# Four copies of x into the output spread over the first units, the last behind a column gather, and the third tile's gather ahead of spreading the weights

## The chip, the core and the metric

The kernel runs on one core of a Trainium2 chip. Times are device microseconds of that core for one whole execution. Engines are TensorE (PE, its weight loads PEld), VectorE (DVE), ScalarE (ACT), GpSimd (POOL) and SyncE (SP). SP, ACT and POOL issue DMA transfers; indirect ones (gathers, and adds into rows of the output) come from POOL.

## The reference

4,096 tokens of 256 numbers go through a mixture of experts with a residual. Eight experts, each a three-layer network (256 to 512 to 512 to 256), two of them per token by a gate; cut to what matters:

```python
xn = rms_w * (x * rsqrt(mean(x * x) + EPS))
gate = xn @ wg_W + wg_b + (genre_embed @ gg_W + gg_b)
topk_w, topk_i = top_k(softmax(gate), 2)
cw = sum(one_hot(topk_i, E) * topk_w[..., None], axis=-2)      # a weight per token and expert
h1 = relu(einsum('bsh,ehm->bsem', x, W1) + b1)
h2 = relu(einsum('bsem,emn->bsen', h1, W2) + b2)
out_e = einsum('bsen,enh->bseh', h2, W3) + b3
return x + einsum('bseh,bse->bsh', out_e, cw)
```

## The kernel before, in words

Only the chosen pairs of token and expert are computed. Tokens lie as 128 partitions with 32 columns; the first 8 columns are part A, the other 24 part B. The gate of part A is computed first, and from it eight tiles of 128 tokens, one for each expert: **units 0 to 7** (E is 8). While these run, VectorE works out the gate of part B, sorts the remaining pairs into tiles by expert, and makes up units of four, two or one tiles, **unit 8 (E) and following**. How many units of which size there are is chosen at run time among prepared programs; the first ones have four tiles.

Each tile needs its rows of x (an indirect gather by token number into `xg`, `xgE` or a part of `big`), the gate weights of its tokens (a gather of 8 numbers per token into `cg`, from the table `cwdA` or `cwdR` that the kernel has written to DRAM: the *column gather*, `gather_cw`), and the expert's weights. After layer 3, `give` multiplies by the token's weight, adds the bias times that weight (`bc`, made by `scaled` from `b3_sb` and `cg`), and an indirect DMA adds the rows into the output (L1328). The output must hold x before: one copy for part A's rows of x (`our[:, 0:NA]`, 1,024 KB, in step 0) and four of 768 KB for part B (`fill`, L1425). Units 0 to 7 add into rows of part A alone and are independent of the four; the first add of unit 8 waits for all of them.

Order is written out by hand (`manual_schedule`): each engine runs its instructions in the order of the program text, and waits on semaphores. `head_step(u)` runs units 0 to 6: layer 1, the transposes of the next tile (L931), a piece of the sorting, layer 3 of the unit before, layer 2. `step(7)` and then `step_fast(u)` run the rest. In those, layers 1 and 2 of a unit with two tiles or more, and layer 3 of four, are computed by a recursion with seven block products instead of eight (classes `Fast` and `Wide`: `p` are matmuls, L1156 and L1246; `c11`, `c12`, `c22` at L1168, L1171, L1174 join products on VectorE; `mix` and `fold` make the sums of blocks; `r1`, `r21`, `r22` are the activations, L1177; copies out of PSUM are L1165 and L1255). `step_fast(u)` overlaps the end of unit u - 1 with the beginning of u. Its first act on VectorE is `scales(u - 1)`, which copies the unit's own columns out of `cg` (L1006); then comes `c22` of layer 2 of unit u - 1.

Queues around the change: SP issues the weights of units 0 to 7 in order (L461), three units ahead, then weights of unit 8 and later whose expert is read from memory (`stream_1`, `stream_3`), the bias rows `b3_sb`, the copies, and for each unit from 9 on the store and reload that reorder its rows (`stow`, L903, and `shuffle`, L910). POOL issues the gathers, the writing of the weight tables (`spread`, L441 to L444) and the output adds. The x gathers of the first three tiles come before step 0; those of tiles 0 and 1 before the table `cwdA` is written, that of tile 2 after it.

Of the kernel before, what the change touches and what calls it, by code (L numbers as in the profile page):

```python
# [52 lines left out]
def kernel(  # L53
# [17 lines left out]
    nc = tc.nc  # L71
    V = nc.vector
    P = 128
    B, S, H = x.shape
# [44 lines left out]
    def buf(pool, shape, name, dt=F32):  # L119
        return pool.tile(shape, dt, tag=name, name=name)  # L120
# [764 lines left out]
            fetches.append(fetch(xgR[u % 2][:, k], xrows, b))  # L885

    NCG = 16
    cgR = buf(run, [P, NCG, E], "cg")

    def gather_cw(u):  # L890
        for k, b in enumerate(tiles(u)):
            cg = cgs[b] = cgR[:, turn_of(u, k) % NCG]
            fetch(cg, (cwdA if b < E else cwdR)[:, :], b)

    xT = buf(run, [P, HC, SLOTS, BT], "xT")
    shs = gTf.rearrange("p (s k f) -> p s k f", s=SLOTS, k=P // SQ)
# [81 lines left out]
    def stream_3(u, engine=mybir.EngineType.Activation):  # L978
        e = expert(u, engine)
        QUEUES[engine].dma_start(w3r[u % RING], W3[e].rearrange("e (c p) h -> p (e c) h", p=P))  # L980
# [385 lines left out]
    def head_step(u, more):  # L1366

        if u + 3 < E:
            gather(u + 3)
        for k in range(3 * u, min(3 * u + 3, E)):  # L1370
            gather_cw(k)
        table(GC * (NCH - 1) * (u == E - 2))
        layer1(u)
        if u == 0:
            load_weights(u + RING, (0,))
            fills.append(nc.sync.dma_start(our[:, 0:NA, :], xr[:, 0:NA, :]))
            load_weights(u + RING - 1, (2,))
            load_weights(u + RING, (1,))
            nc.sync.dma_start(b3_sb[:, 2:4], b3[2:4].unsqueeze(0).to_broadcast([P, 2, H]))
            third_part()  # L1380
        elif u + RING < E:
            load_weights(u + RING, (0,))
        if u == 0:
            pass
        else:
            transpose_x(u + 1)
            stage_1(u + 1)
            if u == E - 2:
                while not fetched:
                    more(1000000)  # L1390
            elif u != 2:
                more(3200)
            if u > 1:
                scaled(u - 1, "A")
            layer3(u - 1)
            if u - 1 + RING < E:
                load_weights(u - 1 + RING, (2,))
            if u + RING < E:
                load_weights(u + RING, (1,))
            if u == 1:  # L1400
                nc.sync.dma_start(b3_sb[:, 4:E], b3[4:E].unsqueeze(0).to_broadcast([P, E - 4, H]))
        table(GC * (u == E - 3))
        if u == 0:
            layer2(u, {1: last_upright, 2: lambda: transpose_x(1)})
            stage_1(1)
            more(3200)
        else:
            more(3200)
            layer2(u)
        if u == 1:  # L1410
            scaled(0, "A")
        if u == E - 2:
            stream_3(E, mybir.EngineType.SP)
            stream_1(E + 1, mybir.EngineType.SP)
            stow(E + 1)
            shuffle(E + 1)
            give(u - 2)
        if u >= 1 and u != E - 3:
            give(u - 1)
        if u == E - 3:  # L1420
            stream_1(E, mybir.EngineType.SP)

    def fill(k):
        i = NA + k * (NB // NF)
        f = nc.sync.dma_start(our[:, i : i + NB // NF, :], xr[:, i : i + NB // NF, :])  # L1425
        for a in sum(adds, []):
            tc.declare_no_dep(f.ins, a.ins, reason="the first E tiles hold tokens of the first part alone")
        fills.append(f)

    def fetches_of(u, last):  # L1430
# [6 lines left out]
    def step(u, last):  # L1437
# [38 lines left out]
        if u == E - 1:  # L1476
            stream_1(E + 2, mybir.EngineType.SP)
            stream_3(E + 1, mybir.EngineType.SP)
            for k in range(NF):
                fill(k)  # L1480
        give(u - 1)
        for _ in folds:
            pass
# [1 line left out]
    def step_fast(u, last):  # L1485

        if u == E:
            transpose_x(u)
        far = fetches_of(u, last)
        follows = u + 1 < last  # L1490
        if follows:
# [189 lines left out]
    with tc.manual_schedule():  # L1681
        first_part()
        gather(0)
        other_loads()
        gather(1)
        second_part()
        pA.spread(cwdA, pA.cw8, 0)
        gather(2)
        other = rest()

        def routing(ns):
            while ns > 0:
                c = next(other, None)
                if c is None:
                    break
                ns -= c

        stage_1(0)
        for u in range(E - 1):
            head_step(u, routing)  # L1700
        for _ in other:
            pass
        for u in range(E - 1, CUT):
            if u == CUT - 2:
                _, (arm,) = nc.values_load_multi_w_load_instructions(
                    nex[0:1, 0:1],
                    min_val=0,
                    max_val=len(ARMS) - 1,
                    skip_runtime_bounds_check_because="the number of a shape of the tail",
                )  # L1710
            elif u == CUT - 1:
                tc.switch_hint({e: arm for e in ENGS}, len(ARMS), "tail")
            steps(u, u + 1, E + NQT + 1)
# [43 lines left out]
```

## Time and profile before

| | before |
|---|---|
| time, median of 3 runs | 452.51 us (452.5 to 453.68) |
| time of the profiled execution | 452.19 us |
| its span, first to last instruction | 450.5 us |
| TensorE busy | 440.3 us (98%) |
| VectorE, ScalarE, GpSimd busy | 368.3, 240.4, 279.8 us |
| moved by DMA | 78.89 MB, 175 GB/s in the mean |
| granted TensorE clock | 0.997 |

Times in the profile are us from the first instruction. A line of the timeline gives start, duration, engine, line of the program, what is written and read, how many instructions, and in brackets how long the engine was idle before and who ended that. A line of a stretch gives its bounds and length, then busy time and count of TensorE, its weight loads, VectorE, ScalarE and GpSimd, the granted clock, the busy share of the DMA engines and GB/s. A line of the DMA list gives what is written and read, the queue, the count, the size and the median us from issue to landing.

### The profile page before, as it was taken

The numbers are of one execution on the slowest core, as the hardware profiler recorded it, in microseconds if no ns is written. First come the engines' busy times: TensorE is split into PE (matmuls) and PEld (weight loads), VectorE is DVE, ScalarE is ACT, GpSimd is POOL, SyncE is SP. The second block draws the span as 40 slices with busy tenths as digits, with TensorE's granted clock in tenths as the row PEclk, the third lists the DMA queues.
The fourth block names the chain that finished last, engine by engine and source line by source line (L and its number), as shares of the span: only waits on it lengthen the run. The fifth ranks groups of instructions, "written<-read, shape, count | busy, mean of one in ns | idle before, by whom it ended". The sixth has DMA issues, their size and how long they took to land. (4 is left out here: it accounts for less than half of the span.)

```text
span 450.5 us, 9264 instructions
## 1 busy us (share of the span) xinstructions
PE 440.3 (98%) x2967; PEld 409.6 (91%) x2967; DVE 368.3 (82%) x964; ACT 240.4 (53%) x569; POOL 279.8 (62%) x234
## 2 busy tenths in 40 slices
PE   8999999999899999999999999999999999999995
PEld 7699999987889898989999999999999889999994
DVE  6897996586897979798988988887977878889962
ACT  5745544345556464728365555563454465655561
POOL 6855436756778878577675647588547456664223
PEclk9999999999999999999999999999999999999998
DMA  8799999495766758374655555567756645766312
GB/s 309 279 350 390 368 368 336 127 316 184 184 173 144 165 110 206 68 171 107 134 125 122 122 120 122 120 152 157 149 136 141 151 133 115 179 172 166 71 18 46
DMA packets 75871, 78.89 MB, mean 175 GB/s; under 512 B 34975, under 2 KB 64002, under 8 KB 75684
## 3 DMA queue, kind: packets, MB, share of 16 engines
q1 hardware_dynamic: 49264, 43.29, 30.3%
q0 software_dynamic: 14912, 17.60, 22.4%
q10 hardware_dynamic: 11636, 17.32, 12.2%
q8 instruction: 25, 0.41, 0.4%
q14 instruction: 34, 0.28, 0.2%
HBM read 62.73 MB, written 20.12 MB: 184 GB/s over the span
## 5 line engine op out<-in xcount | busy, mean ns | idle before, releaser
L1328 POOL DMA_INDIRECT out_dram<-ys,idxR x59 | 95.7, 1622 | 87.2 <-DVE ys L1327 41.7
L1177 ACT ACTIVATE hid<-hid,bb 128x256 f32<-128x256 f32 (+12 forms) x152 | 72.7, 528 | 21.7 <-DVE hid L1174 10.7
L1156 PE MATMUL pb<-hid,big 128*128 128x256 f32 (+7 forms) x456 | 83.3, 326 | 0.0
L864 POOL DMA_INDIRECT cg<-cwdR,idxR x59 | 66.5, 1126 | 18.0 <-issue 17.4
L1156 PEld LDWEIGHTS pb<-hid,big 128*128 128x128 f32 x456 | 71.4, 191 | 4.7 <-issue 0.8
L1278 PE MATMUL pb<-w3r,hid 128*128 128x256 f32 (+1 forms) x256 | 60.7, 381 | 0.0
L1165 ACT COPY q1s<-pb 128x512 f32<-128x512 f32 (+7 forms) x57 | 27.2, 477 | 60.9 <-PE pb L1156 60.3
L1156 PE MATMUL pb<-mixB,big 128*128 128x256 f32 (+7 forms) x304 | 55.5, 326 | 1.1 <-DVE hid L1174 1.1
L1165 ACT COPY big<-pb 128x512 f32<-128x512 f32 (+7 forms) x57 | 27.2, 477 | 51.9 <-PE pb L1156 51.9
L1156 PE MATMUL pb<-hotA,big 128*128 128x256 f32 (+7 forms) x304 | 52.3, 325 | 0.0
L1278 PEld LDWEIGHTS pb<-w3r,hid 128*128 128x128 f32 (+1 forms) x256 | 46.2, 189 | 6.1 <-issue 0.8
L1156 PEld LDWEIGHTS pb<-mixB,big 128*128 128x128 f32 x304 | 47.8, 191 | 4.0 <-DVE hid L1174 1.5
L1156 PEld LDWEIGHTS pb<-hotA,big 128*128 128x128 f32 x304 | 47.2, 191 | 2.7
L1156 PE MATMUL pb<-mixX,iotx 128*128 128x256 f32 (+7 forms) x228 | 46.3, 326 | 0.0
L864 POOL DMA_INDIRECT xgE<-in_x_dram,idxR x31 | 35.2, 1135 | 12.2 <-issue 8.2
L1156 PEld LDWEIGHTS pb<-mixX,iotx 128*128 128x128 f32 x228 | 37.1, 191 | 2.5 <-ACT q1s L1165 0.2
L864 POOL DMA_INDIRECT big<-in_x_dram,idxR x28 | 32.4, 1157 | 8.5 <-issue 7.3
L1177 ACT ACTIVATE hid<-pb,bb 128x256 f32<-128x256 f32 (+7 forms) x76 | 27.6, 414 | 14.7 <-PE pb L1156 11.7
L1156 PE MATMUL pb<-xT,w1r 128*128 128x256 f32 (+7 forms) x152 | 30.8, 325 | 0.0
L1057 PE MATMUL pb<-hid,w2a 128*128 128x128 f32 x256 | 30.4, 276 | 0.0
L1057 PEld LDWEIGHTS pb<-hid,w2a 128*128 128x128 f32 x256 | 29.9, 192 | 0.3
L919 DVE STREAM_TRANSPOSE xT<-gTs 128x256 f32<-128x256 f32 x55 | 29.0, 629 | 0.0
(341 smaller groups left out, 822.6 us busy)
## 6 DMA issues: line engine op xcount, KB each, us to landing
w3r<-in_L_cond_W_dram ACTq DMA_DIRECT2D x17, 512.0 KB, 5.6
w2a<-in_L_cond_W_dram SPq DMA_DIRECT2D x8, 1024.0 KB, 14.3
w1r<-in_L_cond_W_dram ACTq DMA_DIRECT2D x16, 512.0 KB, 3.8
w1r<-in_L_cond_W_dram SPq DMA_DIRECT2D x11, 512.0 KB, 10.0
w3r<-in_L_cond_W_dram SPq DMA_DIRECT2D x10, 512.0 KB, 11.2
big<-in_x_dram SPq DMA_DIRECT2D x8, 512.0 KB, 6.2
gTs<-scr SPq DMA_DIRECT2D x7, 512.0 KB, 4.6
out_dram<-in_x_dram SPq DMA_DIRECT2D x4, 768.0 KB, 9.4
```

Of the source, the lines that this page charges most:

```text
L864: return nc.gpsimd.indirect_dma_start(out=dst, out_offset=None, in_=src, in_offset=bass.IndirectOffsetOnAxis(ap=index(b), axis=0), bounds_ ...
L919: V.transpose(xT[:, :, s0 + k, :].rearrange("p c (b k) -> p k c b", b=SQ), shs[:, s0 + k].rearrange("p k (a c) -> p k c a", a=SQ),)
L1057: nc.tensor.matmul(ph, lhsT=w2[:, m, ts(n, P)], rhs=hid[0][:, m, 0:BT], start=(m == 0), stop=(m == MC - 1))
L1156: nc.tensor.matmul(bank[:, ts(n, self.w)], lhsT=w[:, c, ts(n, P)], rhs=x[:, c], start=new and n == 0 and c == 0, stop=n == HB - 1 and c == ...
L1165: nc.scalar.copy(self.q[(1, 6, 5).index(k)], self.tall(self.X if k == 5 else self.U))
L1177: nc.scalar.activation(out, src, AF.Relu, bias=ww[self.u][1][:, self.l, n : n + 1])
L1278: nc.tensor.matmul(sums(u, k)[0 : cols.stop - cols.start], lhsT=hid[1][:, n, cols], rhs=w3[:, n, :], start=(i == 0), stop=(i == MC - 1))
L1328: add = nc.gpsimd.indirect_dma_start(out=orows, out_offset=bass.IndirectOffsetOnAxis(ap=index(b)[0:n], axis=0), in_=y[0:n], in_offset=None ...
```

## The change

Four edits, all of order. The four copies `fill(0)` to `fill(3)`, before issued one behind the other at the end of `step(7)`, go to the end of `head_step(5)`, into `head_step(6)`, to the old place in `step(7)`, and to the head of `step_fast(8)`; the last waits until the last of unit 8's four column gathers has landed. The bias rows of experts 4 to 7, one load in step 1, become two loads, in steps 2 and 4. The x gather of the third tile goes ahead of writing `cwdA`. The amount of data and the computation are the same.

```diff
     def gather_cw(u):
         for k, b in enumerate(tiles(u)):
             cg = cgs[b] = cgR[:, turn_of(u, k) % NCG]
-            fetch(cg, (cwdA if b < E else cwdR)[:, :], b)
+            columns[u] = fetch(cg, (cwdA if b < E else cwdR)[:, :], b)
...
-            if u == 1:
-                nc.sync.dma_start(b3_sb[:, 4:E], b3[4:E].unsqueeze(0).to_broadcast([P, E - 4, H]))
+            if u in (2, 4):
+                nc.sync.dma_start(b3_sb[:, u + 2 : u + 4], b3[u + 2 : u + 4].unsqueeze(0).to_broadcast([P, 2, H]))
...
         if u == E - 2:
             stream_3(E, mybir.EngineType.SP)
+            fill(1)
             stream_1(E + 1, mybir.EngineType.SP)
...
         if u == E - 3:
             stream_1(E, mybir.EngineType.SP)
+            fill(0)

     def fill(k):
...
+        if k == NF - 1:
+            tc.add_manual_dep(
+                f.ins,
+                columns[E].ins.name,
+                mybir.DependencyInfo(mybir.DependencyClass.Sync, mybir.DependencyReason.DATA),
+                reason="the weight columns of the first unit go first",
+            )
         fills.append(f)
...
             stream_3(E + 1, mybir.EngineType.SP)
-            for k in range(NF):
-                fill(k)
+            fill(2)
         give(u - 1)
...
         if u == E:
             transpose_x(u)
+            fill(3)
         far = fetches_of(u, last)
...
         second_part()
+        gather(2)
         pA.spread(cwdA, pA.cw8, 0)
-        gather(2)
         other = rest()
```

How the rows move. First SP, from unit 8's third weights on (`w3r_88`; `ebt` is the number of the expert, `scr` the scratch of store and reload, `w1r_82`, `w1r_83` and `w3r_86` weights of units 9 and 10). Before:

```order
L980 DMA w3r_88<-in_L_cond_W_dram 128x4x256
L963 TENSOR_LOAD ebt
L976 ISA
L976 DMA w1r_82<-in_L_cond_W_dram 128x1024
L903 DMA scr_186<-big 128x16x64
L910 DMA gTs<-scr_186 128x4x256
```

and further down

```order
L976 DMA w1r_83<-in_L_cond_W_dram 128x1024
L963 TENSOR_LOAD ebt
L980 ISA
L980 DMA w3r_86<-in_L_cond_W_dram 128x4x256
L1425 DMA out_dram<-in_x_dram 128x1536 x4
L903 DMA scr_187<-xgE 128x16x64
L910 DMA gTs<-scr_187 128x4x256
```

In the change, from unit 8's first weights (`w1r_84`) on:

```order
L977 DMA w1r_84<-in_L_cond_W_dram 128x1024
L1428 DMA out_dram<-in_x_dram 128x1536
L964 TENSOR_LOAD ebt
L981 ISA
L981 DMA w3r_88<-in_L_cond_W_dram 128x4x256
L1428 DMA out_dram<-in_x_dram 128x1536
L964 TENSOR_LOAD ebt
L977 ISA
L977 DMA w1r_82<-in_L_cond_W_dram 128x1024
L904 DMA scr_186<-big 128x16x64
```

and where all four stood (with what each row waits for: `DMAHW` is a landing of SP's or ACT's transfers, `DMASW` one of POOL's):

```order
L964 TENSOR_LOAD ebt
L981 ISA
L981 DMA w3r_86<-in_L_cond_W_dram 128x4x256 [waits DMAHW2_49,PE_49]
L1428 DMA out_dram<-in_x_dram 128x1536 [waits DMAHW3_49]
L1428 DMA out_dram<-in_x_dram 128x1536 [waits DMAHW4_49,DMASW0_49]
L904 DMA scr_187<-xgE 128x16x64 [waits DMASW4_49,DMASW5_49,DMASW3_49,DMAHW5_49,DMASW2_49,Pool_49]
```

Two of the copies went up between the weights of units 8 and 9. Two still stand together; the second has a wait for a landing of POOL's, the column gather, and unit 10's store and reload stand behind it.

On POOL, the start of the gathers (`xg_209` to `xg_211` are the rows of tiles 0 to 2, then of 3 to 5). Before:

```order
L864 DMA xg_209<-in_x_dram,idxA 128x256
L864 DMA xg_210<-in_x_dram,idxA 128x256
L441 TENSOR_TENSOR cw8A<-ohA,denA 128x64
L442 TENSOR_TENSOR wA<-ohA,d2A 128x64
L443 TENSOR_TENSOR cw8A<-cw8A,wA 128x64
L444 DMA cwdA<-cw8A 128x64
L864 DMA xg_211<-in_x_dram,idxA 128x256
```

In the change:

```order
L864 DMA xg_209<-in_x_dram,idxA 128x256
L864 DMA xg_210<-in_x_dram,idxA 128x256
L864 DMA xg_211<-in_x_dram,idxA 128x256
L441 TENSOR_TENSOR cw8A<-ohA,denA 128x64
L442 TENSOR_TENSOR wA<-ohA,d2A 128x64
L443 TENSOR_TENSOR cw8A<-cw8A,wA 128x64
L444 DMA cwdA<-cw8A 128x64
```

The third tile's gather went up past the three operations and the write of `cwdA`. Behind both pieces follow the gather of tile 3 and then the column gathers of units 0 to 2, which read `cwdA`.

More of the change, by code (lines that the diff above doesn't have):

```diff
@@ L887 @@
     NCG = 16
+    columns = {}
     cgR = buf(run, [P, NCG, E], "cg")
```

## The prediction

> **What bounds the kernel now.** I read the page first, then the waits of TensorE, then the stretches, then the instructions in order of time around the stretch that stands out. Columns of the waits: who waited for whom, us in total, times, longest.
>
> ```profile
> span 450.5 us, 9264 instructions
> PE 440.3 (98%) x2967; PEld 409.6 (91%) x2967; DVE 368.3 (82%) x964; ACT 240.4 (53%) x569; POOL 279.8 (62%) x234
> ...
> PE pb L1246 <- ACT big L1255: 1.2, 1, 1.2
> PE pb L1156 <- DVE hid L1174: 1.1, 1, 1.1
> PE pb L313 <- PEq L1743: 0.9, 1, 0.9
> PE pb L931 <- DMA xg<-in_x_dram,idxA: 0.7, 2, 0.3
> ...
> 100.00:120.00 20.00, 17.73 (x108) 15.74 (x107) 13.93 (x31) 11.39 (x24) 13.67 (x12) 1.00 0.61 171
> 120.00:140.00 20.00, 20.00 (x109) 18.04 (x109) 17.82 (x39) 10.67 (x22) 16.03 (x14) 1.00 0.73 177
> ```
>
> TensorE has work almost all the time, and no wait occurs more than twice. So a data movement is worth only what it takes out of these few gaps: 1.2 + 1.1 us lie between 100 and 120 us, 0.7 us are two waits for gathered rows of x, the rest is start-up. From 120 us on TensorE is full, so what it gains before then carries through to the last unit. The two large gaps, in order of time (start, duration, engine, line, what, idle before and who ended it):
>
> ```profile
> 92.28 2.52 SPq L1425 DMA_DIRECT2D out_dram<-in_x_dram  x4
> ...
> 94.65 1.39 POOL L864 DMA_INDIRECT cg<-cwdR,idxR  x1 [0.30 <-issue]
> 99.08 1.01 POOL L864 DMA_INDIRECT cg<-cwdR,idxR  x1 [0.30 <-issue]
> 103.28 0.15 DVE L1006 COPY cw<-cg 128x1 f32 x1 [2.47 <-DMA cg<-cwdR,idxR]
> 105.09 0.15 DVE L1006 COPY cw<-cg 128x1 f32 x1 [0.91 <-DMA cg<-cwdR,idxR]
> 105.17 0.69 DVE L1174 TENSOR_TENSOR hid<-pb,big 128x512 f32<-128x512 f32 x1
> 105.91 1.99 PE L1156 MATMUL pb<-mixB,big 128*128 128x256 f32 x8 [1.05 <-DVE hid L1174]
> 109.47 1.03 PE L1156 MATMUL pb<-xT,iotx 128*128 128x256 f32 x4
> 113.56 0.68 DVE L1171 TENSOR_TENSOR hid<-pb,q1s 128x512 f32<-128x512 f32 x1
> 114.27 1.34 ACT L1177 ACTIVATE hid<-hid,bb 128x512 f32<-128x512 f32 x2 [2.42 <-DVE hid L1171]
> 115.52 0.62 ACT L1255 COPY big<-pb 128x256 f32<-128x256 f32 x2
> 116.19 1.16 PE L1246 MATMUL pb<-ohB,mixB 128*128 128x128 f32 x8 [1.22 <-ACT big L1255]
> ...
> out_dram<-in_x_dram SPq DMA_DIRECT2D x4, 768.0 KB, 9.4
> cg<-cwdR,idxR POOLq DMA_INDIRECT x4, 6.2
> ...
> cg<-cwdR,idxR POOLq DMA_INDIRECT x59, 2.4
> ...
> 100.00:102.00 2.00, 2.00 (x11) 1.77 (x10) 0.81 (x2) 0.00 (x0) 0.09 (x1) 1.00 1.07 383
> 104.00:106.00 2.00, 0.95 (x5) 0.49 (x4) 1.07 (x4) 0.11 (x1) 1.70 (x2) 1.00 0.72 195
> ```
>
> SP issues the four copies (768 KB each) at 92.3 to 94.8, just ahead of the four column gathers of unit 8. These take 6.2 us to land where the median of all 59 is 2.4, and the DMA engines are full (1.07, 383 GB/s) until after 104. VectorE needs the columns in its own order, ahead of L1174: it copies the last at 105.09. L1174 then lets TensorE go on at 105.91. VectorE, late by now, shows no idle time until L1171 ends at 114.24; ScalarE waits 2.42 us for that, its copies L1255 come late, and TensorE waits a second time. Both gaps have one cause, the last column.
>
> **The change part by part.**
>
> *Copies ahead of, and behind, the columns.* Now one copy, not four, stands ahead of the gathers at 92.3, the last waits for them, and two went earlier. Let L be the start of the last column's copy on VectorE, now 105.09. The busy run behind it moves with it, so the two gaps, 1.05 + 1.22 = 2.27 us, shrink one for one, and are gone for L = 105.09 - 2.27 = 102.8. Bounds of L: last gather issued 99.08 plus 2.4 gives 101.5 (all 2.27 us gained); plus 6.2 gives 105.3 (nothing). At 383 GB/s a copy (786 thousand bytes) is 2.05 us of transfer, so the three that leave take 6.2 us out of a backlog that ended near 105; it now ends near 99, as the last gather is issued. That is nearer the quiet row; I take 102.1, with 0.6 us added for the output add and the gathers themselves: **-2.27 us**. The data that L1171 reads allow it: the matmuls before it end at 109.47 + 1.03 = 110.5, and I ask for 113.56 - 2.27 = 111.3.
>
> *The last copy waits on SP for the columns.* Behind it on SP stand the store and reload of unit 10's rows:
>
> ```profile
> 113.31 0.40 SPq L903 DMA_DIRECT2D scr<-xgE  x1
> ```
>
> That store waits for gathers anyway until 113.31, 11 us after the columns. Cost nothing; it would cost from the moment the columns landed after 113. The 2.05 us of transfer run from about 102 to 105, when two copies were still in flight before.
>
> *Third tile's gather earlier.*
>
> ```profile
> 18.41 1.03 POOL L864 DMA_INDIRECT xg<-in_x_dram,idxA  x1 [0.31 <-issue]
> 22.32 1.05 POOL L864 DMA_INDIRECT xg<-in_x_dram,idxA  x1 [0.30 <-issue]
> 29.75 0.51 PE L931 MATMUL pb<-ident,xg 128*128 128x128 f32 x2 [0.32 <-DMA xg<-in_x_dram,idxA]
> 28.71 1.03 POOL L864 DMA_INDIRECT cg<-cwdA,idxA  x1 [4.03 <-DMA cwdA<-cw8A]
> 35.92 0.50 ACT L1023 ACTIVATE bc<-b_sb,cg 128x256 f32<-128x256 f32 x1
> 40.40 0.37 ACT L1060 ACTIVATE hid<-pb,vT 128x128 f32<-128x128 f32 x1 [1.92 <-PE pb L1057]
> ```
>
> It goes from 22.32 to right behind the second's (18.41 + 1.03 + 0.31 = 19.75), 2.6 us earlier: the wait of 0.32 us at 29.75 goes (**-0.32 us**). In exchange three POOL operations and the store of the weights move back by 1.03 + 0.31 = 1.34 us, and so do the column gathers behind (28.71 to about 30.1). Their first reader is ScalarE at 35.92; 28.71 + 6.2 + 1.34 = 36.3 makes it some 0.4 us late, and ScalarE idles 1.92 us before 40.40. Nothing reaches TensorE unless the columns are some 2 us later than that.
>
> *Two copies earlier.* One follows the load of unit 8's first weights on SP, one that of its third weights at 73.14. No row shows a copy there. They enter a stretch that is still busy (DMA share 0.77 at 78 to 80):
>
> ```profile
> 73.14 0.38 SPq L980 DMA_DIRECT2D w3r<-in_L_cond_W_dram  x1
> 76.48 1.14 POOL L864 DMA_INDIRECT xgE<-in_x_dram,idxR  x1 [0.30 <-issue]
> 83.61 1.12 PE L931 MATMUL pb<-ident,xgE 128*128 128x128 f32 x8
> 78.00:80.00 2.00, 2.00 (x13) 1.82 (x12) 1.82 (x4) 0.78 (x3) 1.70 (x2) 1.00 0.77 275
> 80.00:82.00 2.00, 2.00 (x19) 1.97 (x19) 1.68 (x3) 0.37 (x1) 1.70 (x2) 1.00 0.31 98
> ```
>
> The two are 4.1 us of transfer, and the engines have room from 80 on (0.31), so the backlog is gone near 84. The last gather of unit 8's rows, issued 76.48, is wanted at 83.61, 7.1 us later. Bounds: as before, no wait, nothing; as slow as the third tile's gather under full load (22.32 to 29.75, 7.4 us), 0.3 us; that plus both copies wholly ahead of it, 7.4 + 4.1 = 11.5 us, 4.4 us. I take nothing: its queue is POOL's, and the copies share the engines with it rather than shut it out.
>
> *The biases of layer 3 in two loads of 256 KB, not one of 512.* The load for units 4 and 5 now follows the weights issued at 45.83:
>
> ```profile
> w2a<-in_L_cond_W_dram SPq DMA_DIRECT2D x8, 1024.0 KB, 14.3
> 60.31 0.52 ACT L1023 ACTIVATE bc<-b_sb,cg 128x256 f32<-128x256 f32 x1
> 63.64 0.37 ACT L1060 ACTIVATE hid<-pb,vT 128x128 f32<-128x128 f32 x1 [2.81 <-PE pb L1057]
> ```
>
> It lands at about 45.83 + 14.3 + 0.7 - 1.4 (half a megabyte less ahead) = 59.4, wanted at 60.31; ScalarE's idle 2.81 us behind that cover an error of 3 us. Nothing gained: no wait of TensorE for weights is in the list. The Trainium skill (DMA: Bandwidth & Descriptors, section Bandwidth) advises the opposite, to bundle transfers to 1 MiB or more, because each has a fixed part of about 2 us; on the path that would make the sum 451.9. No run shown has the split, and by the rows above it would be covered.
>
> *Sum.* -1.05 - 1.22 - 0.32 = -2.59 us. The profiled execution took 452.19 us around its span of 450.5 and becomes 449.6; the median shown, 452.51, becomes **449.9 us**.
>
> **The rivals.** Within 0.3% (1.36 us) a measurement of this kernel can't tell a change from none.
>
> *A: columns as late as before.* Unit 9's and 10's weights and one copy still go ahead of the gathers, so the latency stays 6.2 us; L = 105.3, only the 0.32 us is gained: 452.2. For it: the copies are not the only load at 92. Against it: three of four leave, and the last gather is issued only at 99.08. In between, each us of L past 102.8 costs one. The Trainium skill (DMA: Bandwidth & Descriptors, section Queues, rings and completion order) says that a DMA engine takes turns between the queues that have work, packet by packet; by that rule POOL's gather is slowed while SP's queue holds anything at all, and one copy ahead would do as four do, which is this rival's 452.2 for as long as that one copy lasts. The trace has 6.2 us with SP's queue full, 2.4 as the median, and no row with one copy.
>
> *B: slower, because the early copies make unit 8's rows late.* This is the upper bound above: the last gather lands at 76.48 + 11.5 = 88.0 and TensorE waits 4.4 us at 83.61: 452.5 - 2.6 + 4.4 = 454.3. It makes the change a loss once the rows land 2.6 us after 83.61, at 86.2. For it: the engines are busy up to 80. Against it: the same gathers landed among the weight loads without a wait, and room follows from 80.
>
> *C: part of it.* L near 104, or rows of unit 8 up to 1 us late: 451.0.
>
> **How the numbers follow.** Forecast 65% (449.3 to 450.5), C 13%, A 14%, B 8%. Faster by over 0.3% is the forecast and most of C: 0.76. Same is A and the rest of C: 0.16. Slower 0.08. The range goes down to 449.2 (all gaps and some scatter) and up to 452.2, which takes in C and half of A; the forecast's own range is 449.3 to 450.5.
>
> **What would show it.** TensorE's waits list no L1174 and no L1255 near 105 and 116, and one wait on xg, not two; between 100 and 120 us TensorE is busy 20.00. VectorE's column copies start by 102.8 less what was gained before. Two copies stand before 75, one at 92 and one behind 101. Wrong if TensorE waits at the transposes near 83 (B), if the copies of columns still wait until 105 (A), or if ScalarE is late at the bias products near 36 or 60 and TensorE behind it.

## The result and the profile after

The changed kernel takes **450.73 us** (median of 12 executions, 448.42 to 451.74); the kernel before, on the same chip, 452.64 (12 executions, 450.92 to 454.11). The ratio is **0.995, with a 95% interval of 0.9931 to 0.9969**: faster by 1.4 to 3.1 us. The prediction was 449.9 us, or 2.6 us less than before. Medians here are over all executions; ratios leave out the few that lie more than 1.5% above the fastest of their kernel. The profiled execution of the changed kernel is the fastest of its twelve, 448.42 us; that has to be kept in mind below, since it shows the change at its best.

The page and the list of TensorE's waits over the whole span of the changed kernel. Lines behind the edits have moved by one to three: L1157, L1247, L1175, L1172 and L1256 are L1156, L1246, L1174, L1171 and L1255 of before.

```profile
span 446.7 us, 9272 instructions
...
PE 439.6 (98%) x2967; PEld 409.2 (92%) x2967; DVE 368.4 (82%) x964; ACT 240.0 (54%) x569; POOL 279.4 (63%) x234
```

```profile
PE pb L313 <- PEq L1753: 0.9, 1, 0.9
PE pb L245 <- DMA big<-in_x_dram: 0.4, 1, 0.4
PE pb L932 <- DMA xg<-in_x_dram,idxA: 0.3, 1, 0.3
...
```

Both large waits are gone, and of the two waits for gathered rows one is left. The stretches (bounds, length, busy time of TensorE, its weight loads, VectorE, ScalarE and GpSimd, granted clock, DMA share, GB/s) say the same:

```profile
100.00:120.00 20.00, 20.00 (x121) 18.14 (x120) 16.38 (x38) 12.48 (x26) 16.04 (x14) 1.00 0.63 164
...
78.00:80.00 2.00, 2.00 (x14) 1.82 (x13) 1.93 (x4) 0.31 (x1) 1.70 (x2) 1.00 1.07 421
80.00:82.00 2.00, 2.00 (x21) 2.00 (x20) 1.73 (x4) 0.73 (x2) 1.69 (x2) 1.00 0.99 392
...
100.00:102.00 2.00, 2.00 (x11) 1.77 (x10) 0.67 (x6) 0.27 (x1) 1.70 (x2) 1.00 0.07 2
```

TensorE is busy 20.00 of the 20 us where it was busy 17.73. The column gathers' row in the DMA list (90 to 106 us) shows 5.0 us where it showed 6.2:

```profile
cg<-cwdR,idxR POOLq DMA_INDIRECT x4, 5.0
```

Neither figure is a median of four: the list knows the landing of one of the four gathers in each profile, before of the third, now of the first. From the semaphore records of the traces all four can be timed. Before, they landed 8.6, 7.4, 6.2 and 6.0 us after their issue, now 5.0, 3.6, 2.4 and 2.6 us.

Where the DMA engines moved 383 GB/s between 100 and 102, they now move 2. Part of the backlog ahead of the columns has moved to 78 to 82 us, which was 0.77 and 0.31 full and is now full. The instructions in order of time:

```profile
66.82 0.59 SPq L1428 DMA_DIRECT2D out_dram<-in_x_dram  x1
72.97 1.41 SPq L1428 DMA_DIRECT2D out_dram<-in_x_dram  x1
...
82.98 1.12 PE L932 MATMUL pb<-ident,xgE 128*128 128x128 f32 x8
...
92.24 0.56 SPq L1428 DMA_DIRECT2D out_dram<-in_x_dram  x1
...
95.83 2.10 DVE L920 STREAM_TRANSPOSE xT<-gTs 128x256 f32<-128x256 f32 x4
...
99.15 1.25 POOL L864 DMA_INDIRECT cg<-cwdR,idxR  x1 [0.30 <-issue]
101.75 0.51 SPq L1428 DMA_DIRECT2D out_dram<-in_x_dram  x1
101.76 0.15 DVE L1007 COPY cw<-cg 128x1 f32 x1 [1.30 <-DMA cg<-cwdR,idxR]
...
104.06 1.89 PE L1157 MATMUL pb<-mixB,big 128*128 128x256 f32 x8
...
110.59 0.38 SPq L904 DMA_DIRECT2D scr<-xgE  x1
...
112.86 1.16 PE L1247 MATMUL pb<-ohB,mixB 128*128 128x128 f32 x8
```

The last column is copied at 101.76, not 105.09, and the two matmuls that waited stand without idle time ahead of them (104.06 and 112.86, before 105.91 and 116.19). Unit 8's rows are transposed at 82.98 without a wait, although two copies went ahead.

To see where the 3.77 us between the two profiled executions (452.19 and 448.42) come from, I took the start of each matmul in one trace less its start in the other. The difference changes at a few places only: -0.36 us in start-up (the load of x, which no edit touches), -0.59 at the third tile's transposes, +0.28 at 53.4 (unit 4's second layer), -1.32 at the first gap, -1.37 at the second; it stands at -3.33 us from 116 us on, and some 0.5 us are gained behind the last matmuls.

### The profile page after: what moved, and what is told of

Its sections match the earlier page's. It is cut to its first block, busy times and chain, and to the rows that moved or that the text cites. A ratio compares the mean times of both kernels' runs of the same rounds, so it can differ in the third digit from the quotient of the medians.

```text
span 446.7 us, 9272 instructions
## 1 busy us (share of the span) xinstructions
PE 439.6 (98%) x2967; PEld 409.2 (92%) x2967; DVE 368.4 (82%) x964; ACT 240.0 (54%) x569; POOL 279.4 (63%) x234
## 5 line engine op out<-in xcount | busy, mean ns | idle before, releaser
L1157 PE MATMUL pb<-hid,big 128*128 128x256 f32 (+7 forms) x456 | 83.4, 326 | 0.0
L1157 PEld LDWEIGHTS pb<-hid,big 128*128 128x128 f32 x456 | 71.4, 191 | 4.7 <-issue 0.8
L1157 PE MATMUL pb<-mixB,big 128*128 128x256 f32 (+7 forms) x304 | 55.4, 325 | 0.0
L1157 PE MATMUL pb<-hotA,big 128*128 128x256 f32 (+7 forms) x304 | 52.3, 325 | 0.0
L1157 PEld LDWEIGHTS pb<-mixB,big 128*128 128x128 f32 x304 | 47.9, 191 | 2.6
L1157 PEld LDWEIGHTS pb<-hotA,big 128*128 128x128 f32 x304 | 47.2, 191 | 2.7
L1157 PE MATMUL pb<-mixX,iotx 128*128 128x256 f32 (+7 forms) x228 | 46.3, 326 | 0.0
L1157 PEld LDWEIGHTS pb<-mixX,iotx 128*128 128x128 f32 x228 | 37.1, 191 | 2.5 <-ACT q1s L1166 0.2
L1157 PE MATMUL pb<-xT,w1r 128*128 128x256 f32 (+7 forms) x152 | 30.8, 325 | 0.0
```

The costliest lines, as they stand in the source:

```text
L1157: nc.tensor.matmul(bank[:, ts(n, self.w)], lhsT=w[:, c, ts(n, P)], rhs=x[:, c], start=new and n == 0 and c == 0, stop=n == HB - 1 and c == ...
```

## The experiments

In the kernels of this section lines have moved by one to five against the kernel before. Theory 1 is the prediction's: the last column sets both gaps, a copy costs only what it makes late, and the third tile's gather is worth what its wait was. Its rivals are that the early copies or the moved gather hand a delay on to another place, or that the spread isn't needed since all copies could go behind the columns.

In this section gains and losses at a place are again differences of matmul starts against the profile of before. They run 0.1 to 0.3 us above the idle time that a row shows, since the ends of matmuls are modelled.

**The third tile alone.** The kernel before with this edit only:

```diff
+        gather(2)
         pA.spread(cwdA, pA.cw8, 0)
-        gather(2)
```

> The kernel before with one edit: the third tile's gather goes ahead of spreading the weights. Theory 1 (each edit removes its own wait): TensorE's transposes of the third tile start 0.6 us earlier against their neighbours, as in the changed kernel, where from 27.49 to 29.75 before they took 2.26 us and after 1.79. The two gaps near 105 and 116 stay, with VectorE's last column copy near 104.5 to 105.1. Theory 2 on what is lost again (in the changed kernel TensorE gave back 0.28 us at unit 4's layer 2, near 53.4): if unit 4's second weights simply arrive no earlier, the loss of 0.3 us shows here too, though the bias load is as it was; if the splitting of the bias load made them late, it does not show. Span about 450.2 by the first, 449.9 by the second.

Measured: 452.56 us in one execution, against a median of 452.27 for the kernel before on that chip (23 executions, 450.83 to 455.21), so the time alone says little. TensorE's waits:

```profile
PE pb L1156 <- DVE hid L1174: 1.6, 1, 1.6
PE pb L1246 <- ACT big L1255: 1.2, 1, 1.2
...
PE pb L1057 <- DMA w2a<-in_L_cond_W_dram: 0.7, 1, 0.7
```

The third tile's wait is gone (-0.64 us), and 17 us later TensorE waits 0.7 us for weights that it did not wait for before: unit 3's second layer (L1057) starts 0.9 us later than it would have; the expectation looked for such a loss at unit 4's, near 53.4. In the kernel before TensorE reached that place at 46.63 and the weights had landed at 45.7; now it is there earlier. The gain is taken back there. This happens with the bias rows still in one load, so the split isn't the cause. The first gap is larger than before, 1.6 us, because the last column came later, at 105.53.

**All four copies behind the columns.** The kernel before, with the fills at the head of `step_fast(8)` and the first of them waiting for the last column:

```diff
-            for k in range(NF):
-                fill(k)
         give(u - 1)
...
         if u == E:
             transpose_x(u)
+            for k in range(NF):
+                fill(k)
```

> The kernel before with one edit: all four copies behind the column gathers, none early, the first of them waiting for the last column. Theory 1 (the copies ahead of the columns cause both gaps): the last column copy on VectorE starts near 101.8, both gaps of TensorE go, 2.7 us from start to start. Rival (copies must go early, because behind the columns they meet the gathers, store and reload of unit 10): 8.2 us of transfer run from 102 to 110, unit 10's rows are reloaded 2 to 3 us later than in the changed kernel (120.4), and TensorE waits 1 to 2 us somewhere from 120 to 132. Theory 1 gives a median 2.3 to 2.7 us under the kernel before, the rival 0.5 to 1.5.

Measured: 452.32 us, ratio 1.0002 (0.9984 to 1.0021). No gain at all, though both gaps are gone. Instructions in order of time:

```profile
101.87 2.51 SPq L1426 DMA_DIRECT2D out_dram<-in_x_dram  x4
114.45 0.40 SPq L904 DMA_DIRECT2D scr<-xgE  x1
119.93 0.38 SPq L911 DMA_DIRECT2D gTs<-scr  x1
...
124.68 2.04 DVE L920 STREAM_TRANSPOSE xT<-gTs 128x256 f32<-128x256 f32 x4 [3.73 <-DMA gTs<-scr]
...
125.84 1.13 PE L1157 MATMUL pb<-xT,w1r 128*128 128x256 f32 x4 [0.42 <-DVE xT L920]
129.81 1.99 PE L1157 MATMUL pb<-mixB,big 128*128 128x256 f32 x8 [0.25 <-DVE hid L1175]
140.02 1.16 PE L1247 MATMUL pb<-ohB,mixB 128*128 128x128 f32 x8 [1.19 <-ACT big L1256]
```

The four copies now stand ahead of unit 10's row gathers. These are stored at 114.45 (110.59 in the changed kernel), reloaded at 119.93, and VectorE waits 3.73 us to transpose them. The same chain as before, VectorE late and then ScalarE late, costs 1.2 + 1.5 us of matmul starts, one unit further on. The rival had this chain; the loss is above its 1 to 2 us and reaches to 140 us. So it isn't enough to put the copies behind the columns: they must stay clear of unit 10's rows too.

**The last copy doesn't wait.** The changed kernel without the dependency, so that two copies stand ahead of the columns:

```diff
-        if k == NF - 1:
-            tc.add_manual_dep(f.ins, columns[E].ins.name, ...)
```

> The changed kernel without the wait of the last copy for the columns: two copies stand ahead of the column gathers, not one. Theory 1 with a backlog that is worked off in order (2.05 us a copy): the last column copy starts near 102.5 to 103.5, where one copy gave 101.8 and four 105.1, and the gaps come back by 0 to 0.7 us. Rival (the queues take turns, so one copy ahead does as two do): 101.8 as in the changed kernel, no gap. If one copy gave the floor and the wait is needless, the span is that of the changed kernel within 0.3 us.

Measured: 450.39 us in one execution. VectorE's column copies, and what is left of the gaps:

```profile
102.95 0.67 DVE L1007 COPY cw<-cg 128x1 f32 x4 [2.10 <-DMA cg<-cwdR,idxR]
```

```profile
PE pb L1247 <- ACT big L1256: 1.0, 1, 1.0
...
```

The last column is copied at 103.47. The first gap is gone, of the second 1.0 us is left. Not all of that is the second copy's doing, for the last gather itself was issued later, at 100.30 instead of 99.15:

```profile
100.30 1.01 POOL L864 DMA_INDIRECT cg<-cwdR,idxR  x1 [0.30 <-issue]
```

Why POOL came to it 1.15 us later isn't shown; behind its issue this gather took 3.1 us, in the changed kernel 2.6. So of the 1.7 us by which the column is later, about 0.6 are left for the copy.

The profiles of the two kernels and of the eight runs down to the one without the third tile's move can be set side by side. "Copies" are those issued between 92 us and the columns. "Landed" is the time from the last gather's issue to its landing, from the semaphore records. "Shift" is how much later than before TensorE was just ahead of the first gap (a minus: earlier). "Lost" is what the two gaps together cost in matmul starts, counted against the profiles in which both are wholly gone.

| kernel | copies | last gather issued | landed, us | last column copied (L) | shift | lost |
|---|---|---|---|---|---|---|
| before | 4 | 99.08 | 6.0 | 105.09 | 0 | 2.85 |
| third tile alone | 4 | 99.66 | 5.8 | 105.53 | -0.12 | 3.40 |
| last copy doesn't wait | 2 | 100.30 | 3.1 | 103.47 | 0.02 | 1.26 |
| changed kernel | 1 | 99.15 | 2.6 | 101.76 | -0.63 | 0.15 |
| changed kernel again | 1 | 99.36 | 2.4 | 101.76 | 0.30 | 0 |
| without the third tile's move | 1 | 99.73 | 2.4 | 102.12 | 0.65 | 0 |
| all behind the columns | 0 | 99.40 | 2.5 | 101.88 | -0.40 | 0.03 |
| four early | 0 | 101.40 | 2.4 | 103.85 | 0.37 | 1.24 |
| four early, again | 0 | 99.25 | 3.6 | 102.84 | 0.17 | 0.43 |
| one early, two behind unit 8's rows | 0 | 98.47 | 3.4 | 102.91 | -0.61 | 1.24 |

Two things follow. The loss at both gaps is L less the shift less 102.24 us, to 0.05 us, in each profile where there is any, whatever made L late: both gaps hang on the last column, one for one. And four copies ahead make the last gather land in 6 us, where one or none gives 2.4 to 2.6; but copies aren't the only thing that makes L late. In the last two rows none is near and the gather still takes 3.4 to 3.6 us, with two weight loads of 512 KB issued ahead of it (at 94.9 and 96.0, and at 94.3 and 95.3); in the row of four early it is issued late.

**All four copies early.** The changed kernel with two copies behind unit 8's first weights, two behind its third weights, and none later:

```diff
             stream_3(E, mybir.EngineType.SP)
-            fill(1)
+            fill(2)
+            fill(3)
...
             stream_1(E, mybir.EngineType.SP)
             fill(0)
+            fill(1)
...
             stream_3(E + 1, mybir.EngineType.SP)
-            fill(2)
...
             transpose_x(u)
-            fill(3)
```

> The changed kernel with all four copies early: two behind unit 8's first weights, two behind its third weights, none near the columns and no wait for them. This doubles what was suspected to make unit 8's rows late. If the copies hold up POOL's gathers in full (4.1 us more than in the changed kernel, where the last gather of unit 8's rows took 5.9 us to land from 75.84): it lands near 86 and TensorE waits about 3 us at the transposes near 83; 2 to 3 us slower than the changed kernel. If the queues share the engines: it lands at 82 to 83, TensorE waits under 0.5 us, the store of unit 9's rows near 85.5 goes at 86 to 88, and the last column copy starts at about 101.4; the time is that of the changed kernel within 0.5 us.

Measured: 449.11 us, ratio 0.9934 (0.9914 to 0.9955); ten of twelve executions between 448.42 and 449.84. The profiled one was the slowest, 453.74, and shows two losses. No wait stands at unit 8's rows, which the first part of the expectation feared. But the last gather of the columns is issued late (101.40), VectorE copies the last column at 103.85, and 1.0 us of the second gap is there, with no copy near:

```profile
103.85 0.15 DVE L1007 COPY cw<-cg 128x1 f32 x1 [1.32 <-DMA cg<-cwdR,idxR]
...
114.95 1.16 PE L1247 MATMUL pb<-ohB,mixB 128*128 128x128 f32 x8 [0.97 <-ACT big L1256]
```

The larger loss, 2.9 us of matmul starts, lies behind 116 us: a reload of 512 KB. First the DMA list of 112 to 122 us (last number: median us to landing), then VectorE, then TensorE's waits.

```profile
w3r<-in_L_cond_W_dram ACTq DMA_DIRECT2D x1, 512.0 KB, 8.8
gTs<-scr SPq DMA_DIRECT2D x1, 512.0 KB, 9.1
```

```profile
126.81 2.03 DVE L920 STREAM_TRANSPOSE xT<-gTs 128x256 f32<-128x256 f32 x4 [4.23 <-DMA gTs<-scr]
```

```profile
PE pb L1247 <- ACT big L1256: 2.2, 2, 1.2
PE pb L1058 <- DMA w2a<-in_L_cond_W_dram: 0.9, 1, 0.9
...
PE pb L1157 <- DVE xT L920: 0.6, 1, 0.6
```

The reload of unit 10's rows took 9.1 us; in the changed kernel it took 5.2, and 6.75 in that kernel's second profile, which cost TensorE nothing. The 7.7 us of the run without the third tile's move cost 1.3 us, the 9.1 here 2.9, by the same chain as in the run with all copies behind.

**The same two kernels again, on one chip.**

> The changed kernel once more, beside the two variants below on one chip. Every theory: between 449.4 and 451.8, because the runs so far lay between 448.4 and 451.7 with a median of 450.7. The last copy of the columns on VectorE should again be issued near 101.8 us, and both gaps of TensorE (L1156 waiting for L1174, L1246 waiting for L1255) should again be absent.

> All four copies early once more (two behind unit 8's first stream of rows, two behind its third), none near the columns. Theory 1 (what counts is that no copy shares the queues with the columns and that unit 10's gathers stay clear of copies too): both gaps of TensorE absent, last column copy on VectorE by 102.8 us, time 0.8 to 2 us under the changed kernel, 448.6 to 450. Theory 2 (early copies hold up the rows of unit 8 and 9, which hands the delay on to the columns): column copy at 103.5 us or later as in the one profile of this variant, the second gap still there with some 1.1 us, and no time under that of the changed kernel. The reload that took 9.1 us in that profile should take 4 to 5 us if it was a chance collision.

Measured: changed kernel 451.13 us, ratio 0.9965 (0.9942 to 0.9988); four early 450.31 (8 executions), ratio 0.9952 (0.992 to 0.9984). The changed kernel's profile again has neither gap, and the last column again at 101.76. It loses 0.8 us of starts at another place, though, where it had lost nothing the first time: TensorE waits for unit 6's rows, gathered at 53.42.

```profile
59.73 0.51 PE L932 MATMUL pb<-ident,xg 128*128 128x128 f32 x2 [0.56 <-DMA xg<-in_x_dram,idxA]
```

The better time of four early is not confirmed: its interval lies over that of the changed kernel. Its profile shows what it pays. VectorE and TensorE with four early:

```profile
98.49 2.05 DVE L920 STREAM_TRANSPOSE xT<-gTs 128x256 f32<-128x256 f32 x4 [1.77 <-DMA gTs<-scr]
102.66 0.33 DVE L1007 COPY cw<-cg 128x1 f32 x4
113.94 1.16 PE L1247 MATMUL pb<-ohB,mixB 128*128 128x128 f32 x8 [0.16 <-ACT big L1256]
```

VectorE doesn't wait for the columns any more; it comes to them late, because it waited 1.77 us for **unit 9's** rows (transposed at 98.49, in the changed kernel at 95.83). The last column itself landed only at 102.82, so both were late at once. Part of the delay has moved to another transfer that VectorE needs.

**One copy early, two behind unit 8's rows, one behind the columns.**

```diff
             stream_3(E, mybir.EngineType.SP)
-            fill(1)
             stream_1(E + 1, mybir.EngineType.SP)
+            fill(1)
+            fill(2)
...
             stream_3(E + 1, mybir.EngineType.SP)
-            fill(2)
```

Here `fill(1)` waits until the last row gather of unit 8 has landed.

> One copy early, two behind unit 8's row gathers (the first of them waits until the last of those rows has landed), one behind the columns. Theory 1 (copies cost only what they make late): nothing lies ahead of the columns that is still in flight when they are issued, columns as early as in the changed kernel (last copy on VectorE near 101.8 us), no gap; within 0.5 us of the changed kernel, 450.2 to 451.2. Theory 2 (the wait on the queue holds back unit 9's rows behind it, since they are issued by the same engine): TensorE waits for unit 9's transposed rows, and the time is 1 to 3 us above the changed kernel.

Measured: 450.13 us, ratio 0.9947 (0.9929 to 0.9966). The order of time:

```profile
81.77 1.17 SPq L1430 DMA_DIRECT2D out_dram<-in_x_dram  x2
...
93.36 0.38 SPq L911 DMA_DIRECT2D gTs<-scr  x1
...
98.55 2.07 DVE L920 STREAM_TRANSPOSE xT<-gTs 128x256 f32<-128x256 f32 x4 [2.62 <-DMA gTs<-scr]
102.73 0.33 DVE L1007 COPY cw<-cg 128x1 f32 x4
...
113.98 1.16 PE L1247 MATMUL pb<-ohB,mixB 128*128 128x128 f32 x8 [0.97 <-ACT big L1256]
```

Both expectations were half right: the time is that of the changed kernel, as theory 1 had it, but the last column is copied at 102.9, not 101.8, and not because of the columns, the last of which had landed at 101.83. Unit 9's reload starts at 93.36 (89.46 in the changed kernel), VectorE waits 2.62 us for it, and 0.97 us of the second gap is back. TensorE does not wait at unit 9's rows, which theory 2 expected; the delay reaches it through VectorE's order.

**The changed kernel without the third tile's move.**

> The changed kernel without the third tile's move: the copies are spread, the gather stays behind the spreading of the weights. Theory 1 (the third tile's gain is taken back by the arrival of the weights, as its run alone showed): the same time as the changed kernel within 0.4 us, the third tile's wait of 0.6 us back at 28 us and no later wait of TensorE for unit 3's or unit 4's weights of the second layer. Theory 2 (the gain of the third tile stays to the end): 0.6 us above the changed kernel.

Measured: 450.25 us, ratio 0.9952 (0.9927 to 0.9978), on the same chip as the three runs above: no slower than with the move. Its profile, though, doesn't show the reason that theory 1 gave. Without the move, the third tile's transposes started without the wait of before (29.12 against 29.75, the rows having landed 1 us sooner, for which the trace shows no reason), and the loss near 46 us was the largest of all, 1.4 us of starts. TensorE and VectorE:

```profile
47.21 1.02 PE L1058 MATMUL pb<-hid,w2a 128*128 128x128 f32 x7 [1.16 <-DMA w2a<-in_L_cond_W_dram]
...
124.31 2.04 DVE L920 STREAM_TRANSPOSE xT<-gTs 128x256 f32<-128x256 f32 x4 [2.69 <-DMA gTs<-scr]
```

So the weights' arrival changes by itself. In the ten profiles so far these weights landed between 45.3 and 47.1 us, with the same order of loads. 15 of the 16 parts of such a transfer land within about 2 us of each other, the last one 0.1 to 1.7 us behind the fifteenth (here 45.4 and 47.1 us). In each of these profiles a load of 16 KB of program text, 1.0 to 1.2 us long, begins between 44.1 and 45.1, as these weights land. Whether it holds up the sixteenth part isn't shown, since the trace doesn't say which engine moved which packet.

With the tile's gather moved, TensorE began this layer at 45.7, 46.4, 46.6, 46.9, 46.0, 46.7 and 45.7 us (seven profiles, mean 46.3), in the kernel before at 46.63. Of the 0.6 us gained at 29 us, about 0.3 arrives, and that is no more than start-up gave by itself.

**Four more, which settle little.** They ran on another chip, where the kernel before takes 464.13 us (35 executions, 460.54 to 471.54), 12 us more than on the others. The changed kernel itself did not run there, so the times below are set against the kernel before, and the expectations, which are given against the changed kernel, can't be judged by them.

The first part's copy behind unit 3's weights (and unit 5's gather ahead of the first add):

```diff
             load_weights(u + RING, (0,))
-            fills.append(nc.sync.dma_start(our[:, 0:NA, :], xr[:, 0:NA, :]))
             load_weights(u + RING - 1, (2,))
             load_weights(u + RING, (1,))
+            fills.append(nc.sync.dma_start(our[:, 0:NA, :], xr[:, 0:NA, :]))
```

> The changed kernel with the first part's copy of x (1 MB, 2.7 us of the queues between the landings at 38.8 and 41.5) put behind unit 3's weights of the second layer instead of ahead of them; unit 5's row gather goes ahead of the first add into the output, which now waits longer for that copy. Theory 1 (the head is set by the arrival of the weights, which takes back the third tile's gain): unit 3's second-layer weights land at 42.7 to 44.5 instead of 45.3 to 47.1, TensorE no longer waits for them near 46 us, and what it has then gained over the kernel before (0.9 us) stays up to unit 4's second layer at 53.4, where 0 to 0.6 us may be lost again; time 0 to 0.7 us under the changed kernel. Theory 2 (the losses near 46 us come from elsewhere, as from TensorE's own order): the step there stays at 0.3 to 1.3 us. Rival: the late add holds up POOL and makes unit 5's or 6's rows late, and the time is 0.3 to 1 us above the changed kernel.

ScalarE's two weight loads 4 us later:

```diff
             f.r22()
-            streams(u, last)
+            if u > E + 1:
+                streams(u, last)
...
             g.p(k)
+            if u == E + 1 and k == 1:
+                streams(u, last)
```

> The changed kernel with two weight loads of 0.5 MB each, which ScalarE issues at 114.5 and 115.5 beside unit 10's reload at 115.2, issued some 4 us later. Theory 1 (what is left of the scatter behind 116 us is unit 10's reload, which takes 3.9 to 9.1 us when it collides with those loads): the reload takes 3.7 to 4.5 us, lands by 120, TensorE has no wait near 140, and the time is 0 to 0.6 us under the changed kernel with fewer runs above 451. Theory 2 (the reload's length comes from POOL's row gathers or from chance alone): still 5 us or more, and the same time. The moved loads land by 127 and are read from 129 on, so they should cost nothing.

The bias rows in one load:

```diff
-            if u in (2, 4):
-                nc.sync.dma_start(b3_sb[:, u + 2 : u + 4], ...)
+            if u == 1:
+                nc.sync.dma_start(b3_sb[:, 4:E], ...)
```

> The changed kernel with the last four bias rows in one load at unit 1 as in the kernel before, instead of two loads at units 2 and 4. Theory 1 (the split is worth nothing): within 0.4 us of the changed kernel, no new wait of TensorE between 50 and 70 us. Theory 2 (the smaller load at that place is what lets the weights of unit 4 and 5 keep up with an earlier TensorE): those weights land 0.7 to 1.5 us later, TensorE waits for them at 53 or 60 us, and the time is 0.4 to 1 us above the changed kernel.

And four early with the first two of these edits:

> All four copies early (as in the variant that took 449.1 and 450.3), the first part's copy behind unit 3's weights, and the two weight loads at 114.5 later. Theory 1: the three places where the changed kernel and its variants still lose by chance (unit 3's weights near 46 us, the columns near 103 us, unit 10's reload near 120 us) are covered at once; 448.2 to 449.5, about 1.5 us under the changed kernel, with few runs above 450. Theory 2 (early copies make the columns late when the queues are fuller): the last column copy on VectorE at 102.8 to 103.9, the second gap of 0.2 to 1.1 us back, and 449.5 to 450.5.

| | median, us | ratio to before on that chip |
|---|---|---|
| first part's copy later | 465.54 | 1.0009 (0.9969 to 1.005) |
| two loads later | 462.71 | 0.9987 (0.9949 to 1.0025) |
| bias rows in one load | 460.95 | 0.9963 (0.9923 to 1.0003) |
| together | 466.01 | 1.0046 (1.0012 to 1.0079) |

One of the twelve executions with the bias rows in one load took 1,176.79 us, for which there is no trace; its ratio is without it.

In all four profiles TensorE stops for 2.2 to 3.8 us near 36 us and once more, for 1.3 to 5.7 us, between 128 and 158. Behind each of these stops but the shortest it runs on at half its clock, for 3.4 or 6.8 us. The first profile, TensorE in order of time and then the stretches:

```profile
38.36 0.71 PE L1048 MATMUL pb<-xT,w1r 128*128 128x128 f32 x4 [3.14 <-issue]
```

```profile
34.00:36.00 2.00, 1.22 (x11) 1.02 (x10) 1.89 (x4) 0.37 (x1) 1.39 (x3) 1.00 1.08 384
36.00:38.00 2.00, 0.00 (x0) 0.00 (x0) 1.59 (x3) 0.06 (x1) 1.81 (x3) 1.00 1.04 356
38.00:40.00 2.00, 0.88 (x5) 0.69 (x6) 0.00 (x0) 0.90 (x4) 0.77 (x1) 0.74 1.07 355
40.00:42.00 2.00, 2.00 (x10) 2.00 (x11) 0.73 (x3) 1.31 (x5) 0.00 (x0) 0.50 1.10 409
```

TensorE starts nothing for 3.14 us and the profile shows nothing that it waits for; ScalarE stops there too. In two of the four profiles the wait is put down to ScalarE (L1061), which itself waits there for nothing that the profile names. In the four profiles TensorE is then 6.0 to 7.4 us later than in the changed kernel's first profile at the place that the first edit was to help, and more behind it, so these edits weren't tested: unit 3's weights did land earlier (42.5 us in the first, 43.2 in the last, forecast 42.7 to 44.5), but with TensorE late nothing waits for them. The last, which joins the three remedies, is slower there than the kernel before, against what I expected; why is open. For the bias rows the one thing that can be said is that with one load the time is as far under the kernel before, 0.9963, as with two on the other chips, 0.995 and 0.9965; the interval reaches just past 1.

No variant beat the changed kernel beyond the intervals.

## Why the prediction was right, point by point

The median fell by 1.91 us, the ratio says 2.26 (1.4 to 3.1); the prediction said 2.6, so it is inside, and the direction and the place were right. By its own steps:

*Both gaps hang on the last column.* Right. I took L = 102.1; it came at 101.76, next to the quiet bound of 101.5. That the copies made it late is shown by the run with all copies behind, where nothing else was changed and both gaps went, and that both gaps follow it, one for one, by the table of ten profiles. The 6.2 us that I took for the four gathers, and the 2.4 us for all 59, rest on one known landing of four and eight of 59; the last gather, which sets the bound, took 6.0, so the bound hardly moves.

*The threshold, L under 102.8.* Too late by 0.6 us. By the table it is 102.24 for a TensorE that arrives as before, and a TensorE that is earlier lowers it by as much as it is earlier. The two gaps were worth 2.85 us of matmul starts, and I counted their idle time, 1.05 + 1.22 us; the ends of matmuls, from which idle time is counted, are modelled in the trace. So in the changed kernel's profile, where TensorE came 0.63 us earlier, L = 101.76 is 0.15 us over the bound, although no idle time is listed: the gain was 2.70 there, not 2.85. What is gained ahead tightens the bound behind; the prediction says so at its end, but its sum doesn't use it.

*The last copy's wait on SP, nothing.* Right. SP comes to unit 10's store at 110.59, 9 us after the copy at 101.75, and earlier than the 113.31 of before. That all four copies at this place would have cost 2.7 us I had not seen: I priced the wait of the one, not the room behind it.

*Two early copies, nothing, and rival B.* Right: no wait at 82.98. The DMA engines were full until 82 (0.55 busy from 82 to 84), where the forecast had "near 84". The mechanism of B exists, though, one unit later: in the variants with copies ahead of unit 9's rows these came late, and in two of their profiles that reached TensorE through VectorE (0.16 and 0.97 us of idle time).

*The third tile, -0.32 us.* This is the term that failed. Its wait went, and TensorE gained 0.59 us there in the profile, but the gain did not reach the end in the mean: unit 3's weights arrive up to 1.2 us too late in starts for a TensorE that is earlier (in two of seven profiles not too late at all), and in three profiles something more was lost, 0.28 us at unit 4's weights, 0.8 and 0.3 us at unit 6's rows. Alone the edit gave 452.56 in one execution against 452.27, and without it the change took 450.25 against 451.13 with it. "No wait of TensorE for weights is in the list" was true of before, and was not enough: unit 3's weights had landed at 45.7 for a use at 46.63, a slack of 0.9 us that the list of waits can't show.

*The split of the bias rows, nothing.* Not contradicted: one load on the other chip gave 0.9963. In one of the seven profiles with two loads TensorE waits near 60 us, for unit 6's rows (0.56 us idle), and in another it starts 0.3 us late there. In the first those rows took 6.3 us to land, 5.8 to 6.0 in the other six and 5.8 in the three with one load, so whether the split has a part in it isn't shown. The Trainium skill (DMA: Bandwidth & Descriptors, section Bandwidth) advises larger transfers; no loss from the two smaller ones is to be seen.

*Rival A.* It fell. The Trainium skill's rule that queues with work take turns (DMA: Bandwidth & Descriptors, section Queues, rings and completion order) fits what was measured: the last gather took 6.0 and 5.8 us with four copies, 3.1 with two, and 2.4 to 2.6 with one or none where no weights were still on their way (3.4 to 3.6 where they were). It decides nothing against the change because the one copy was all but through: it landed 0.2 to 1.0 us after the last gather was issued, and the gather needed 2.4 us anyway.

*The size.* The forecast was 449.9 and the median 450.73. That it is so near is in part luck, since errors of both signs went into the sum: the gaps were worth some 0.4 to 0.6 us more than I counted, the third tile's 0.32 came to nothing, and three places that lose in some executions were left out, unit 3's weights (0 to 1.4 us of starts), unit 6's rows (0.8 us in one profile of the changed kernel, none in the other) and unit 10's reload (0 in most profiles, 1.3 and 2.9 us in two of them). How the 0.8 us divides between them stays open.

## What to carry to other kernels

A list of waits shows where an engine lost time, not how near the next loss is: before counting a gain on an engine that is 98% busy, follow it down the line and look, at each later place that needs a transfer, how long ahead of its use that transfer landed. A transfer with no deadline of its own belongs in stretches where nothing with a deadline stands right behind it: four copies in one place cost TensorE time at the columns or at unit 10's rows. Spread over four places, or two and two early, they gained the same within the intervals, and two and two early still touched unit 9's rows. And where the difference sought is 0.2% and single executions spread by 0.7%, one profile is one draw: here one taken alone would have shown 3.8 us for a change worth 1.9. What did hold from profile to profile is the relation behind a wait, here between L, TensorE's arrival and the loss.

## What was not expected of the hardware

The same loads landed at quite different times from one execution to the next: a megabyte of weights between 45.3 and 47.1 us with the same loads in the same order ahead of it, mostly by the last of 16 parts, and a reload of 512 KB beside two weight loads and four gathers in 3.8 to 9.1 us. On one chip, TensorE and ScalarE stopped for 1.3 to 5.7 us with no cause that the profile names. After TensorE had started nothing for 3.14 us its granted clock was 0.50 for 6.8 us, and after stops of 2.17 and 2.37 us for 6.8 and 3.4 us, where gaps of 1.0 to 1.3 us left it at 1.00. The Trainium skill (TensorE: Matmul & The Clock Gate, Part 1) has TensorE at half rate after an idle window of about 3.4 us; here shorter stops were followed by it too. From these figures, as an estimate, a stop of 2 to 4 us costs 1.7 to 3.4 us more by the clock, and in the four profiles from that chip the two stops with what follows them make most of what they lose against the changed kernel's first profile.
